# A gated long convolution inside a decoder kernel: nine block products a head, the pair products on GpSimd, the skip path from the pairs' diagonal

## The chip, the cores and the metric

The kernel runs on one core of a Trainium2 chip, as one program in one launch. The time is the device time of that program in microseconds (us). The kernel before was run three times; a profiled execution of it was taken beside them. TensorE is called PE in the profile, its weight load PEld, VectorE DVE, ScalarE ACT, GpSimd POOL and SyncE SP.

## The reference

The program is a two-layer decoder on x [8, 256, 512] (8 sequences, 256 tokens, 512 values), each sublayer followed by a residual add and a layernorm: differential attention, **a gated long convolution with the context**, a routed feed-forward of 8 experts (top 2), self attention, cross attention, routed attention. All values are float32. The change is in the second sublayer, which treats the 256 tokens as channels, 32 heads of 8, and convolves along the 512 values:

```python
def _L0_xattn_ref(v, k, bias, x1, x2, num_heads):   # v = x, x1 = x2 = context, k [32, 512]
    vr, x1r, x2r = (t.reshape(B, H, num_heads, L) for t in (v, x1, x2))
    kv = vr[:, :, :, None, :] * x2r[:, :, None, :, :]          # 8 x 8 pairs a head
    y = irfft(rfft(kv, n=2 * L) * rfft(k, n=2 * L)[None, :, None, None, :])[..., :L]
    y = y + kv * bias.reshape(H, num_heads)[None, :, :, None, None]
    return jnp.einsum('bhijl,bhil->bhjl', y, x1r).reshape(B, D, L)

x = _layernorm(x + _L0_xattn_ref(x, L0_xattn_k, fside_S2_0, ctx_2048, ctx_2048, 8))
```

The convolution is causal, so y at l is the sum over m <= l of k[l - m] times the pair at m. The `bias` term comes, after the sum over i, to c_j times the sum over i of bias_i x_i c_i.

## The kernel before

**Layout.** `long_conv` works on turned data: `xh[i]` and `ch[i]` hold x and the context for token half i as 128 partitions x 4 blocks (KB) x 8 sequences x 128 tokens, so 128 neighbouring values of L lie on the partitions and L is 4 blocks of 128. `xh[0]`, `ch[0]`, `xh[1]`, `ch[1]` reuse large buffers whose names in the profile are those of other stages (`first_h`, `w_l1a`). `turn` (helper L166) transposes the sixteen token tiles of x into `xh`: eight even ones in front of the heads, four odd ones after head 0 and four after head 1. The context is loaded from `ctx_d` in DRAM, four DMAs a half (L551).

**One head** (loop over h = 0 to 31, 16 a half). The pairs kv[k] (L571) are 128x512 products (8 sequences x 8 x 8 pairs), one for each block k of L; k = 0, 1, 2 are made on VectorE, k = 3 on GpSimd. Within 128x128 blocks the causal convolution is a lower block triangle with one Toeplitz block T0 to T3 for each distance: y_lb is the sum over k <= lb of T(lb-k) kv[k], ten block products. The blocks of a head are slices of `wt` [128, 512], which a DMA reads from the DRAM tile `filters` (L565) by an access pattern that steps back one value a row. `project` (L172) accumulates each y_lb in a PSUM bank `ps_y` (six banks); a float32 product of 128x128 by 128x512 is issued as two matmul instructions. VectorE multiplies each ps_y by the context into z (L606, three buffers) and sums over i into `yc` (L609).

**The skip path of a head.** GpSimd makes u = x c (L579) and u times bias (L580), VectorE sums over i into `us` (L587), GpSimd makes r = c us (L589), r + x (L595) and, last, x = r + yc in place (L610). These are 128x256 operations.

**The routing.** When the sixteen heads of half 0 are done, the router of the next sublayer is run for its eight token tiles between the heads of half 1: each tile is transposed back on TensorE (`pt_c`, L789), copied by ScalarE to a row tile `xn` (L795), its moments taken by VectorE (L145, L146) and normed (L771), and router logits come from `ps_r` (L178) and `pt_r` (L190). Then `choose` (VectorE: softmax, top two), `send` (L842, L843, then L856: sixteen indirect DMAs, issued on GpSimd, that write the rows to their experts' slots), `table` (L893: block tables) and `meanwhile` (the first expert blocks) follow. Half 1 is routed after head 31, beside the first expert products (`pg`, `pu` on L172).

**What sets the order.** Each engine works through its own instruction stream in order. The framework's scheduler places the instructions of all engines by a plan of its own; nothing in this stage is ordered by hand. SP issues the loads and stores of the whole program from one in-order queue. Pools with a number of buffers (`bufs`) make the next writer of a tile wait until the readers of the buffer are done.

```python
for k in range(KB):
    (nc.gpsimd if k == KB - 1 else nc.vector).tensor_tensor(kv[:, k], x_i, c_j, ALU.mult)
...
for lb in range(KB):
    project(ps, lambda k: wt[:, (lb - k) * P : (lb - k + 1) * P], lambda k: kv[:, k], n=lb + 1)
    nc.vector.tensor_tensor(z, ps, c_i, ALU.mult)
    nc.vector.tensor_reduce(yc[:, lb], z, AX.X, ALU.add)
```

Of the kernel before, what the change touches and what calls it, by code (L numbers as in the profile page):

```python
# [50 lines left out]
def decoder_kernel(ctx: ExitStack, tc: tile.TileContext, a: dict, out: bass.AP):  # L51
# [37 lines left out]
    filters = dram.tile([NH, P, KPAD], F32, tag="filters", name="filters")  # L89

# [6 lines left out]
    def spread_filters():  # L97
        n = NH // 4
        for h in range(0, NH, n):
# [3 lines left out]
            )  # L103

# [132 lines left out]
    class Pipeline:  # L237
# [3 lines left out]
        def __init__(self):  # L241
            self.steps = []
# [15 lines left out]
    def diff_attention():  # L258
# [26 lines left out]
        load_x(range(TPG, NT))  # L285
        spread_filters()
# [34 lines left out]
        clear_slots(wpool)  # L321

# [212 lines left out]
    def long_conv(router, load_experts, xh, ch, ps_t, meanwhile):  # L535
# [5 lines left out]
        with ExitStack() as st:  # L541
# [18 lines left out]
            for h in range(NH):  # L560
                i, at = divmod(h * NHEAD, P)
                hs = slice(at, at + NHEAD)
                xv, cv = xh[i], ch[i]
                wt = work.tile([P, D], F32, tag="wt", name="wt", bufs=3)
                nc.sync.dma_start(out=wt, in_=toeplitz(h))  # L565
                if h == 2:
                    load_experts()

                kv = work.tile([P, KB, B, NHEAD, NHEAD], F32, tag="kv", name="kv")
                for k in range(KB):  # L570
                    (nc.gpsimd if k == KB - 1 else nc.vector).tensor_tensor(  # L571
                        kv[:, k],
                        xv[:, k, :, hs].unsqueeze(2).broadcast_to(shape),
                        cv[:, k, :, hs].unsqueeze(3).broadcast_to(shape),
                        ALU.mult,
                    )

                u = work.tile([P, KB, B, NHEAD], F32, tag="u", name="u")
                nc.gpsimd.tensor_tensor(u, xv[:, :, :, hs], cv[:, :, :, hs], ALU.mult)  # L579
                nc.gpsimd.tensor_tensor(  # L580
                    u,
                    u,
                    sk[:, h * NHEAD : (h + 1) * NHEAD].unsqueeze(1).unsqueeze(1).broadcast_to([P, KB, B, NHEAD]),
                    ALU.mult,
                )
                us = work.tile([P, KB, B], F32, tag="us", name="us")
                nc.vector.tensor_reduce(us, u, AX.X, ALU.add)  # L587
                r = work.tile([P, KB, B, NHEAD], F32, tag="r", name="r")
                nc.gpsimd.tensor_tensor(  # L589
                    r,  # L590
                    cv[:, :, :, hs],
# [24 lines left out]
                if h == NH // 2 - 1:  # L616
                    tiles, choose, send, table = route(ps_t, xv, i)
                    for f in tiles:
                        f(work)
# [1354 lines left out]
```

## Time and profile before

| what | us |
|---|---|
| median of three runs | 2171.05 (2167.81 to 2173.65) |
| profiled execution, its own time | 2169.91 |
| its span in the profile | 2168.2 |
| convolution, first to last product | 483.18 to 782.64 |
| busy in the span: PE, DVE, ACT, POOL | 2012.0, 1275.9, 603.4, 827.9 |

The profile is of one execution. A busy share is an average over stages with different limits, so a stage is read in windows of its own. In a group line, the number after the bar is the busy time, then the mean of one in ns, then the idle time of the engine just in front of it and what ended that. The row of a matmul is longer than the distance between two starts, since they overlap. In a line of the timeline, the first number is the start in us from the start of the span, the second its length, and the brackets give the idle time before it and what released it. PEclk is the share of its full clock that TensorE was granted.

### The profile page before, as it was taken

How to read it: one execution, taken by the hardware profiler on the slowest of the kernel's cores; microseconds unless marked ns; L12 is line 12 of the kernel's file. 1: busy time of each engine (PE TensorE's matmuls, PEld its weight loads, DVE VectorE, ACT ScalarE, POOL GpSimd, SP SyncE). 2: the span in 40 equal slices, each digit the busy share in tenths (PEclk: the TensorE clock that was granted, in tenths of full speed). 3: DMA queues.
4: the chain of work that ended last, by engine and by line, in shares of the span. 5: the costliest groups of instructions: out<-in, count | busy, mean ns of one | idle time of the engine just before them, and what ended most of it. 6: DMA issues, size and time to landing. Idle time of an engine off the chain costs nothing. (4 is left out here: it accounts for less than half of the span.)

```text
span 2168.2 us, 36044 instructions
## 1 busy us (share of the span) xinstructions
PE 2012.0 (93%) x15094; PEld 1221.4 (56%) x15094; DVE 1275.9 (59%) x1935; ACT 603.4 (28%) x765; POOL 827.9 (38%) x919
## 2 busy tenths in 40 slices
PE   8979999879998999999959999999999999999995
PEld 6645655444443455566536665656877875444443
DVE  4677777658888963222244756456344343576787
ACT  4545556510010022111113333430110111333332
POOL 2677777736557622000034544333000000142343
PEclk9999999999999999999989999999999999999998
DMA  6899702235133153142141211002100100000000
GB/s 228 333 402 400 290 2 60 84 100 189 29 117 121 34 165 137 64 146 65 42 151 30 69 34 46 2 2 98 39 20 20 32 8 1 1 6 16 11 21 30
DMA packets 110033, 197.58 MB, mean 91 GB/s; under 512 B 7088, under 2 KB 30768, under 8 KB 109872
## 3 DMA queue, kind: packets, MB, share of 16 engines
q1 hardware_dynamic: 104752, 178.49, 23.3%
q0 software_dynamic: 5120, 16.78, 2.3%
q8 instruction: 121, 1.98, 0.4%
q14 instruction: 40, 0.33, 0.0%
HBM read 93.54 MB, written 112.20 MB: 95 GB/s over the span
## 5 line engine op out<-in xcount | busy, mean ns | idle before, releaser
L1357 DVE RECIPROCAL rsum<-ps_pv 128x256 f32<-128x256 f32 x128 | 224.4, 1753 | 241.2 <-PE ps_pv L1349 241.2
L172 PE MATMUL ps_y<-kv,wt 128*128 128x512 f32 x640 | 281.5, 599 | 5.7 <-POOL kv L571 2.7
L1313 ACT ACTIVATE pT<-ps_k 128x1536 f32<-128x1536 f32 x128 | 185.8, 1451 | 278.5 <-PE ps_k L1305 272.1
L1253 DVE TENSOR_REDUCE neg<-rows 128x12 f32<-128x1536 f32 x128 | 223.0, 1742 | 46.6 <-POOL rows L1244 46.6
L1314 POOL TENSOR_SCALAR_AFFINE_SELECT pT<-pT 128x1024 f32<-128x1024 f32 x128 | 141.2, 1103 | 245.8 <-ACT pT L1313 245.7
L1242 ACT COPY rows<-ps_q 128x1536 f32<-128x1536 f32 x128 | 184.2, 1439 | 175.9 <-PE ps_q L1233 123.4
L1244 POOL TENSOR_SCALAR_AFFINE_SELECT rows<-rows 128x1024 f32<-128x1024 f32 x128 | 141.8, 1108 | 231.8 <-ACT rows L1242 231.6
L172 PEld LDWEIGHTS ps_y<-kv,wt 128*128 128x128 f32 x640 | 121.3, 192 | 157.9 <-issue 139.3
L1324 POOL TENSOR_TENSOR pT<-pT 128x512 f32<-128x512 f32 x112 | 145.6, 1300 | 9.4
L205 PE MATMUL ps_f<-xT,w_l1a 128*128 128x256 f32 x512 | 127.4, 396 | 12.2 <-ACT xT L218 12.2
L1159 POOL DMA_INDIRECT w_l1x<-ys,slots x32 | 33.0, 1032 | 263.4 <-DMA ys<-y_m 255.7
L205 PE MATMUL ps_t<-w_l1f,xT 128*128 128x512 f32 x256 | 123.0, 615 | 0.0
L205 PEld LDWEIGHTS ps_f<-xT,w_l1a 128*128 128x128 f32 x512 | 95.6, 194 | 33.4 <-ACT xT L218 14.3
L1071 PE MATMUL po_m<-dn,hT 128*128 (+1 forms) x216 | 98.7, 593 | 1.0 <-ACT hT L1061 1.0
L140 POOL TENSOR_SCALAR rstd<-bn_mv 128x1 f32<-128x1 f32 x80 | 16.7, 209 | 210.0 <-DVE bn_mv L146 204.2
L1349 PE MATMUL ps_pv<-pT,ones_v 128*32 128x256 f32 (+1 forms) x1152 | 84.5, 375 | 8.2 <-POOL pT L1324 7.9
L609 DVE TENSOR_REDUCE yc<-z 128x64 f32<-128x512 f32 x128 | 86.1, 674 | 5.7 <-POOL w_l1a L610 5.3
L1233 PE MATMUL ps_q<-kz,qT 32*128 32x128 f32 x1536 | 62.2, 292 | 16.8 <-ACT pT L1313 13.4
L172 PE MATMUL pg<-gu,xT_b 128*128 x216 | 71.0, 465 | 3.8 <-ACT xT_b L218 3.8
L1233 PEld LDWEIGHTS ps_q<-kT,qT 32*128 32x128 f32 x1536 | 49.8, 190 | 42.9 <-issue 20.5
L1233 PEld LDWEIGHTS ps_q<-kz,qT 32*128 32x128 f32 x1536 | 49.8, 190 | 42.0 <-ACT pT L1313 28.0
L1050 DVE TENSOR_TENSOR h_b<-h_b,pg 128x352 f32<-128x352 f32 x36 | 18.8, 521 | 92.1 <-ACT h_b L1049 90.6
(338 smaller groups left out, 3692.0 us busy)
## 6 DMA issues: line engine op xcount, KB each, us to landing
xs<-zero SPq DMA_DIRECT2D x8, 4352.0 KB
ys<-zero SPq DMA_DIRECT2D x8, 4352.0 KB
filters<-in_L_xattn_k SPq DMA_DIRECT2D x4, 2560.0 KB
first_h<-xs SPq DMA_DIRECT2D x36, 256.0 KB
ys<-y_m SPq DMA_DIRECT2D x36, 256.0 KB
gu<-in_L_ffn_gate_up_proj SPq DMA_DIRECT2D x3, 2816.0 KB
wt<-filters SPq DMA_DIRECT2D x32, 256.0 KB
x<-in_x SPq DMA_DIRECT2D x16, 256.0 KB
```

Source lines behind the costliest of these rows:

```text
L172: nc.tensor.matmul(ps, lhsT=lhsT(k), rhs=rhs(k), start=(k == 0), stop=(k == n - 1))
L205: nc.tensor.matmul(ps[0], lhsT=lhsT(k), rhs=rhs(k), start=(k == 0), stop=(k == KB - 1))
L609: nc.vector.tensor_reduce(yc[:, lb], z, AX.X, ALU.add)
L1071: nc.tensor.matmul(po, lhsT=hT[:m, i, :], rhs=dn[i][:m, bass.ds(e, 1), :], start=(i == 0), stop=(i == len(FCH) - 1),)
L1233: nc.tensor.matmul(block[:, s, j, :], lhsT=q(rows, c, b * S + i * P, P), rhs=k(rows, c, b * S + keys * P, P), start=True, stop=True,)
L1242: nc.scalar.copy(d.rearrange("p j s k -> p s j k"), block)
L1244: nc.gpsimd.affine_select(out=rows, in_=rows, compare_op=ALU.is_ge, fill=-FAR, base=0, pattern=[[0, 8], [-1, P]], channel_multiplier=1,)
L1253: return lambda: nc.vector.tensor_reduce(neg[u // upb % 2][:, :, :, c], d, AX.X, ALU.max, negate=True)
L1313: nc.scalar.activation(p[:, 0:3].rearrange("p j s q -> p s j q"), block, AF.Exp)
L1314: nc.gpsimd.affine_select(out=p[:, 0:2].rearrange("p j s q -> p (j s) q"), in_=p[:, 0:2].rearrange("p j s q -> p (j s) q"), compare_op=ALU ...
L1324: nc.gpsimd.tensor_tensor(p[:, 3], p[:, 1], p[:, 2], ALU.add)
L1357: nc.vector.reciprocal(r, ps[:, 1, :])
```

## The change

Nine products a head take the place of ten. T2 is applied once to kv[0] + kv[1] (`both`): its result serves y2 (which needs T2 kv[0]) and y3 (which needs T2 kv[1]). It is made first, in y2's PSUM bank, ScalarE copies it to an SBUF tile `common`, and what is too much or missing is made good by products with differences of filter blocks: y2 = common + (T1 - T2) kv[1] + T0 kv[2], added in the same bank, and y3 = common + (T3 - T2) kv[0] + T1 kv[2] + T0 kv[3], where VectorE adds `common` to the finished bank in the next head's step (`last_sum`). The differences are made once from the 32 filter rows on GpSimd (`filter_changes`), spread to a DRAM tile `changes` of 8.4 MB (`spread_changes`, on SP after the zeros of `clear_slots`), and a second DMA a head loads `wd` [128, 384] (two buffers).

All four pair products of a head and the sum `both` are made on GpSimd, one head ahead (`kv` has two buffers, `both` and `common` one); head 0's pairs are on VectorE. The skip path takes the products x_i c_i from the diagonal of kv: VectorE multiplies it by the bias into `u`, 128x256 a head. Four heads form a group: one `skip_sums` on VectorE (128x1024 to 128x128) and `weighted`, `residual`, `done` on GpSimd (128x1024 each), the last three one in each of the first three steps of the next group. z has one buffer.

For heads 2 to 14 and 16 to 30 the order on PE, DVE and Pool is the written one (`manual_schedule`): `step`. The eight token tiles of half 0's routing stand one in each of steps 16 to 23, in front of the head's products; `choose`, `send`, `table` and `meanwhile` are handed to the scheduler in front of steps 24 to 27. Heads 0, 1, 15 and 31 are left to the scheduler. The loops for the odd turns stand where they stood in the source. The core of the diff:

```diff
+    changes = dram.tile([NH, P, D], F32, tag="changes", name="changes")
...
+    def filter_changes(pool):
+        f = pool.tile([NH, KPAD], F32, tag="f_rows", name="f_rows")
+        nc.sync.dma_start(out=f, in_=a["L0_xattn_k"])
+        d = pool.tile([NH, 2, S], F32, tag="f_diff", name="f_diff")
+        second = f[:, 2 * P : 2 * P + S]
+        nc.gpsimd.tensor_tensor(d[:, 0], f[:, P : P + S], second, ALU.subtract)
+        nc.gpsimd.tensor_tensor(d[:, 1], f[:, 3 * P : 3 * P + S], second, ALU.subtract)
+        return d
+    def spread_changes(d):
+        nc.sync.dma_start(
+            out=changes[:, :, :],
+            in_=d.rearrange("h j c -> h (j c)").unsqueeze(1).broadcast_to([NH, P, D]),
+        )
+    def toeplitz_changes(h):
+        flat = changes[h].rearrange("m c -> (m c)")
+        return flat[P : P + P * (D - 1)].rearrange("(m c) -> m c", c=D - 1)[:, : D - P]
...
         load_x(range(TPG, NT))
+        d_filters = filter_changes(wpool)
         spread_filters()
...
         clear_slots(wpool)
+        spread_changes(d_filters)
...
+            GH = 4
+            GT = GH * NHEAD
+            over = [P, KB, B, GT]
+            class Group:
+                def __init__(self, g):
+                    self.i, at = divmod(g * GT, P)
+                    self.hs = slice(at, at + GT)
+                    self.xg, self.cg = xh[self.i][:, :, :, self.hs], ch[self.i][:, :, :, self.hs]
+                    self.yc = work.tile(over, F32, tag="yc", name="yc")
+                def skip_products(self, head):
+                    if head.h % GH == 0:
+                        self.u = work.tile(over, F32, tag="u", name="u")
+                    same = head.kv.rearrange("p k b j i -> p k b (j i)")[:, :, :, :: NHEAD + 1]
+                    part = sk[:, head.h * NHEAD : (head.h + 1) * NHEAD]
+                    at = head.h % GH * NHEAD
+                    nc.vector.tensor_tensor(
+                        self.u[:, :, :, at : at + NHEAD],
+                        same,
+                        part.unsqueeze(1).unsqueeze(1).broadcast_to([P, KB, B, NHEAD]),
+                        ALU.mult,
+                    )
+                def skip_sums(self):
+                    self.us = work.tile([P, KB, B, GH], F32, tag="us", name="us", bufs=1)
+                    nc.vector.tensor_reduce(
+                        self.us,
+                        self.u.rearrange("p k b (n i) -> p (k b) n i", i=NHEAD),
+                        AX.X,
+                        ALU.add,
+                    )
+                def weighted(self):
+                    self.r = self.u
+                    four = [P, KB * B, GH, NHEAD]
+                    nc.gpsimd.tensor_tensor(
+                        self.r.rearrange("p k b (n i) -> p (k b) n i", i=NHEAD),
+                        self.cg.rearrange("p k b (n i) -> p (k b) n i", i=NHEAD),
+                        self.us.rearrange("p k b n -> p (k b) n").unsqueeze(3).broadcast_to(four),
+                        ALU.mult,
+                    )
+                def residual(self):
+                    nc.gpsimd.tensor_tensor(self.r, self.r, self.xg, ALU.add)
+                def done(self):
+                    nc.gpsimd.tensor_tensor(self.xg, self.r, self.yc, ALU.add)
+            class Head:
+                def __init__(self, h, group):
+                    self.h = h
+                    self.i, at = divmod(h * NHEAD, P)
+                    self.hs = slice(at, at + NHEAD)
+                    self.xv, self.cv = xh[self.i], ch[self.i]
+                    at = h % GH * NHEAD
+                    self.yc = group.yc[:, :, :, at : at + NHEAD]
+                    self.wt = work.tile([P, D], F32, tag="wt", name="wt", bufs=3)
+                    nc.sync.dma_start(out=self.wt, in_=toeplitz(h))
+                    self.wd = work.tile([P, D - P], F32, tag="wd", name="wd")
+                    nc.sync.dma_start(out=self.wd, in_=toeplitz_changes(h))
+                    self.kv = work.tile([P, KB, B, NHEAD, NHEAD], F32, tag="kv", name="kv")
+                def pairs(self, k):
+                    (nc.gpsimd if self.h else nc.vector).tensor_tensor(
+                        self.kv[:, k],
+                        self.xv[:, k, :, self.hs].unsqueeze(2).broadcast_to(shape),
+                        self.cv[:, k, :, self.hs].unsqueeze(3).broadcast_to(shape),
+                        ALU.mult,
+                    )
+                def add_pairs(self):
+                    self.both = work.tile(shape, F32, tag="both", name="both", bufs=1)
+                    nc.gpsimd.tensor_tensor(self.both, self.kv[:, 0], self.kv[:, 1], ALU.add)
+                def block(self, n):
+                    return self.wt[:, n * P : (n + 1) * P]
+                def change(self, n):
+                    return self.wd[:, n * S : n * S + P]
+                def sum_of(self, ps, *parts, first=True):
+                    if first:
+                        ps = psum.tile([P, B, NHEAD, NHEAD], F32, tag="y", name="ps_y")
+                    for k, (wb, xb) in enumerate(parts):
+                        nc.tensor.matmul(
+                            ps,
+                            lhsT=wb,
+                            rhs=xb,
+                            start=first and k == 0,
+                            stop=k == len(parts) - 1,
+                            skip_group_check=True,
+                        )
+                    return ps
+                def weighted_sum(self, lb, y):
+                    z = work.tile([P, B, NHEAD, NHEAD], F32, tag="z", name="z", bufs=1)
+                    nc.vector.tensor_tensor(
+                        z, y, self.cv[:, lb, :, self.hs].unsqueeze(2).broadcast_to(shape), ALU.mult
+                    )
+                    nc.vector.tensor_reduce(self.yc[:, lb], z, AX.X, ALU.add)
+                def products(self):
+                    kv, of, at = self.kv, self.block, self.change
+                    y2 = self.sum_of(None, (of(2), self.both))
+                    self.common = work.tile(shape, F32, tag="common", name="common", bufs=1)
+                    nc.scalar.copy(self.common, y2)
+                    y0 = self.sum_of(None, (of(0), kv[:, 0]))
+                    y1 = self.sum_of(None, (of(1), kv[:, 0]), (of(0), kv[:, 1]))
+                    self.sum_of(y2, (at(0), kv[:, 1]), (of(0), kv[:, 2]), first=False)
+                    y3 = self.sum_of(
+                        None, (at(1), kv[:, 0]), (of(1), kv[:, 2]), (of(0), kv[:, 3])
+                    )
+                    self.y = [y0, y1, y2, y3]
+                def last_sum(self):
+                    nc.vector.tensor_tensor(self.y[3], self.y[3], self.common, ALU.add)
+                    self.weighted_sum(3, self.y[3])
+            def step(h, routed=lambda: None):
+                head = heads[h]
+                before = heads[h - 1] if h % (NH // 2) else None
+                behind = heads[h + 1] if h + 1 < NH else None
+                group, at = groups[h // GH], h % GH
+                passed = groups[h // GH - 1] if h % (NH // 2) >= GH else None
+                if before:
+                    before.last_sum()
+                routed()
+                head.products()
+                if behind:
+                    behind.pairs(0)
+                    behind.pairs(1)
+                    behind.add_pairs()
+                head.weighted_sum(0, head.y[0])
+                group.skip_products(head)
+                if passed and at < 3:
+                    (passed.weighted, passed.residual, passed.done)[at]()
+                if behind:
+                    behind.pairs(2)
+                    behind.pairs(3)
+                head.weighted_sum(1, head.y[1])
+                head.weighted_sum(2, head.y[2])
+                if at == GH - 1:
+                    group.skip_sums()
+            order = {mybir.EngineType.PE, mybir.EngineType.DVE, mybir.EngineType.Pool}
+            groups = [Group(0)]
+            heads = [Head(0, groups[0])]
+            for k in range(KB):
+                heads[0].pairs(k)
+            heads[0].add_pairs()
+            parts, free = [], []
             for h in range(NH):
-                i, at = divmod(h * NHEAD, P)
-                hs = slice(at, at + NHEAD)
-                xv, cv = xh[i], ch[i]
-                wt = work.tile([P, D], F32, tag="wt", name="wt", bufs=3)
-                nc.sync.dma_start(out=wt, in_=toeplitz(h))
+                if h + 1 < NH:
+                    if (h + 1) % GH == 0:
+                        groups.append(Group((h + 1) // GH))
+                    heads.append(Head(h + 1, groups[-1]))
                 if h == 2:
                     load_experts()
-
-                kv = work.tile([P, KB, B, NHEAD, NHEAD], F32, tag="kv", name="kv")
-                for k in range(KB):
-                    (nc.gpsimd if k == KB - 1 else nc.vector).tensor_tensor(
-                        kv[:, k],
-                        xv[:, k, :, hs].unsqueeze(2).broadcast_to(shape),
-                        cv[:, k, :, hs].unsqueeze(3).broadcast_to(shape),
-                        ALU.mult,
-                    )
-
-                u = work.tile([P, KB, B, NHEAD], F32, tag="u", name="u")
-                nc.gpsimd.tensor_tensor(u, xv[:, :, :, hs], cv[:, :, :, hs], ALU.mult)
-                nc.gpsimd.tensor_tensor(
-                    u,
-                    u,
-                    sk[:, h * NHEAD : (h + 1) * NHEAD].unsqueeze(1).unsqueeze(1).broadcast_to([P, KB, B, NHEAD]),
-                    ALU.mult,
-                )
-                us = work.tile([P, KB, B], F32, tag="us", name="us")
-                nc.vector.tensor_reduce(us, u, AX.X, ALU.add)
-                r = work.tile([P, KB, B, NHEAD], F32, tag="r", name="r")
-                nc.gpsimd.tensor_tensor(
-                    r,
-                    cv[:, :, :, hs],
-                    us.unsqueeze(3).broadcast_to([P, KB, B, NHEAD]),
-                    ALU.mult,
-                )
-                nc.gpsimd.tensor_tensor(r, r, xv[:, :, :, hs], ALU.add)
-                yc = work.tile([P, KB, B, NHEAD], F32, tag="yc", name="yc")
-                for lb in range(KB):
-                    ps = psum.tile([P, B, NHEAD, NHEAD], F32, tag="y", name="ps_y")
-                    project(
-                        ps,
-                        lambda k: wt[:, (lb - k) * P : (lb - k + 1) * P],
-                        lambda k: kv[:, k],
-                        n=lb + 1,
-                    )
-                    z = work.tile([P, B, NHEAD, NHEAD], F32, tag="z", name="z", bufs=3)
-                    nc.vector.tensor_tensor(
-                        z, ps, cv[:, lb, :, hs].unsqueeze(2).broadcast_to(shape), ALU.mult
-                    )
-                    nc.vector.tensor_reduce(yc[:, lb], z, AX.X, ALU.add)
-                nc.gpsimd.tensor_tensor(xv[:, :, :, hs], r, yc, ALU.add)
+                last = h == NH // 2 - 1 or h == NH - 1
+                if h < 2 or last:
+                    step(h)
+                else:
+                    if not parts and free:
+                        free.pop(0)()
+                    with tc.manual_schedule(engines=order):
+                        step(h, parts.pop(0) if parts else lambda: None)
+                if last:
+                    heads[h].last_sum()
+                    groups[h // GH].weighted()
+                    groups[h // GH].residual()
+                    groups[h // GH].done()
                 if h < 2:
                     for t in range(h * PH + 1, (h + 1) * PH, 2):
                         turn(t)
                     if h == 1:
                         x_first.close()
                 if h == NH // 2 - 1:
-                    tiles, choose, send, table = route(ps_t, xv, i)
-                    for f in tiles:
-                        f(work)
-                    for f in (choose, send, table, meanwhile):
-                        f()
+                    tiles, choose, send, table = route(ps_t, xh[0], 0)
+                    parts = [lambda f=f: f(work) for f in tiles]
+                    free = [choose, send, table, meanwhile]
             return route(ps_t, xh[1], 1)
```

## The prediction

> **What bounds the stage now.** I read the busy shares first, then the groups by line, then the table of windows through the convolution, then the timeline around its worst gap. The changed stage is the convolution, from its first product at 483.18 us to its last at 782.64.
>
> ```profile
> PE 2012.0 (93%) x15094; PEld 1221.4 (56%) x15094; DVE 1275.9 (59%) x1935; ACT 603.4 (28%) x765; POOL 827.9 (38%) x919
> ...
> L172 PE MATMUL ps_y<-kv,wt 128*128 128x512 f32 x640 | 281.5, 599 | 5.7 <-POOL kv L571 2.7
> ```
> TensorE carries the span, and the product group waits only 5.7 us in all. The shares average over stages, so I go to the stage itself (columns: window, its length, busy time and count of PE, PEld, DVE, ACT, POOL, granted clock, DMA share, GB/s).
>
> ```profile
> 523.00:563.00 40.00, 40.00 (x100) 18.18 (x99) 35.79 (x58) 0.00 (x0) 22.45 (x27) 1.00 0.24 87
> ...
> 643.00:683.00 40.00, 36.04 (x86) 15.20 (x85) 39.82 (x117) 0.26 (x1) 22.68 (x24) 1.00 0.39 137
> 683.00:723.00 40.00, 37.26 (x81) 16.07 (x80) 30.68 (x51) 0.00 (x0) 37.00 (x44) 0.91 0.28 93
> ```
> In the plain heads TensorE never stops, VectorE has 4 us of 40 free and GpSimd 17. Only where the first half's routing is mixed in does TensorE lose time.
>
> ```profile
> 681.99 1.90 POOL L856 DMA_INDIRECT xs<-xn,slots  x1 [0.30 <-DVE kv L571]
> ...
> 689.27 0.96 POOL L856 DMA_INDIRECT xs<-xn,slots  x1 [0.30 <-issue]
> ...
> 691.51 1.07 POOL L571 TENSOR_TENSOR kv<-w_l1a 128x512 f32<-128x512 f32 x1
> 692.63 11.89 PE L172 MATMUL ps_y<-kv,wt 128*128 128x512 f32 x20 [2.74 <-POOL kv L571]
> ```
> Sixteen dispatch transfers hold GpSimd from 668.68 to 690.25, the pair product queued behind them comes late, and TensorE idles. The windows after it show the clock:
>
> ```profile
> 690.00:692.00 2.00, 0.00 (x0) 0.00 (x0) 0.98 (x2) 0.00 (x0) 1.98 (x4) 0.99 0.45 168
> 692.00:694.00 2.00, 1.36 (x2) 0.83 (x3) 2.00 (x3) 0.00 (x0) 2.00 (x3) 0.50 0.22 74
> 694.00:696.00 2.00, 2.00 (x3) 0.67 (x2) 2.00 (x4) 0.00 (x0) 2.00 (x4) 0.50 0.76 264
> 696.00:698.00 2.00, 2.00 (x4) 0.76 (x3) 0.52 (x2) 0.00 (x0) 2.00 (x4) 0.50 0.90 281
> 698.00:700.00 2.00, 2.00 (x5) 0.84 (x4) 0.00 (x0) 0.00 (x0) 2.00 (x4) 0.80 0.13 45
> ```
> After about 3.1 us of rest TensorE runs some 6 us at half clock, 3.0 us lost. A long stall costs itself plus 3 us.
>
> **1. The products.** Forty matmul instructions start in 17.43 us, 0.43 us each (a row's 592 ns overlaps the next). A block product is two, a head ten products, 8.6 us. Nine are 7.74. All four pair products, the copy and the extra add must hide behind 7.74 (below). 32 x 0.86 = **-27.5**.
>
> **2. Do the others keep up with 7.74 us a step?** GpSimd: four pairs at 1.07 (L571's row on the first half; back to back 1.02) are 4.27; `both` has no row, bounds 1.07 and L1324's 1.30 (contiguous 128x512), taken 1.30, the same shape; per four heads `weighted` 1.9, `residual` and `done` 2.35 each (the 128x256 rows, 0.63 and 0.72, scaled by L1324 to 128x1024; bounds 1.1, the affine select of that shape, and 2.55), 1.65 a head. Sum 7.2. VectorE: four multiplies (0.68) and four reduces (0.67), chained because z has one buffer: 774.09 to 774.82 is 0.73 for a chained step, so 5.8; the add into PSUM 0.73 (bounds 0.60 independent, 1.10 with twice the PSUM traffic); the skip product 0.7 (bounds 0.33, half a pair product, and 1.3, when GpSimd holds it up as it holds L571: 0.85 mean against 0.67 at best); group reduce 1.2 / 4 = 0.3. Sum 7.5. ScalarE's copy, 0.6, has 1.9 us before product five wants the bank. All hidden, so 0, but thinly: each 0.1 us over 7.74 costs 3 us, up to 32 heads. The two DMAs for `wd` and `wt` need 0.6 us each of an idle queue: 0.
>
> [...]
>
> **3. The start.** SP works in order. Before, w_l1a's four loads from ctx_d were issued at 436 us; in the built program they stand behind first_h's, released at 473.14 in both, and ahead of the first `wt`. 2.1 MB at 0.30 MB/us (the rate of first_h and `wt`: 2.36 MB in 10 us is 0.24; gu's 0.415 is the other bound): 5.1 to 8.9, taken **+6.9**. Head 0's pairs hide in it. The eight odd turns and ps_cs, 0.88 + 2.5 + 0.81 us on TensorE's timeline between heads 0 and 2 before, now lie in that wait: **-4.2**. The rest of 2.6 to 4 us may halve the clock: 0 to 3, taken **+1.5**. The write of `changes` (8.4 MB at 11.3 us per 4.35 MB, 22 us) ends well before cx is used (75 us of cover): 0; f_rows and two subtractions stand before GpSimd's first busy stretch: 0.
>
> **4. The half boundary.** In the built order VectorE meets head 15's skip product and the group reduce in the middle of step 14, in front of z2. That product waits for GpSimd's fourth pair of head 15, which cannot start before head 13 frees its kv buffer: pairs, `both`, `done` and pairs end 8.1 us into the step, VectorE was free at 5.1. z2 then ends at 11.5, 3.8 into step 15; y1 of head 15 takes z2's bank and is due at 1.7: 2.05 stall, and product five waits 0.4 for the copy behind the late add: 2.45. Then tile 0's transpose stands on TensorE between heads 15 and 16 and waits for `done` of the group, which waits for last_sum(15). VectorE ends z2's reduce 4.5 into step 15, last_sum(14) (add, multiply, reduce) at 6.7, three multiplies and reduces at 11.1, last_sum(15) at 13.3; `done` takes 2.35, so 15.7. TensorE is through at 7.74 + 2.45 = 10.2: 5.5 idle, less 0.57 that the same transpose waited before, plus 3.0 of clock. **+10.4**. Head 31 repeats the 2.45 on its way in; its long tail lies beside an expert's 6.1 us of products: **+2.4**.
>
> **5. Dispatch and routing.** Now the sixteen transfers stand between the third and fourth pair of head 27. They begin 7.0 us into step 26, take 20.3 (1.27 each), and the pair 1.07: 28.4 into step 26. TensorE has products up to 7.74 + 6.9 = 14.6: idle 14. Then `both` of head 28 needs two more pairs and itself: +2. Clock +3, the chained tail on VectorE 1.3, and steps 16 to 23, where the norm (0.69 + 0.18 + 0.55 a tile) comes on top of VectorE's 7.5, 1.5 (they get 1.3 us of transposes as well). 21.8, against 1.16 + 0.53 + 0.58 + 0.76 + 0.86 + 2.74 + 3.0 = 9.6 before, all of which goes. **+12.2** (0 if the transfers start 14 us earlier; 16 if slots come 3 us late).
>
> [...]
>
> **Sum.** -27.5 + 6.9 - 4.2 + 1.5 + 10.4 + 2.4 + 12.2 = +1.7. On the profiled execution's 2169.91 (span 2168.2) that is 2171.6; it lies 1.1 below the median 2171.05 of the runs, so 2172.8 in the runs. No change is 2164.5 to 2177.6, 0.3% of the median, about what a measurement of this kernel can tell.
>
> **Rivals.**
> *The stalls stay as short as before.* If `slots` are ready a step earlier than GpSimd gets to them, or the transfers start behind less of the pairs, part 5 costs its old 9.6, and the rest under 3 us at the start keeps the clock: 2172.8 - 12.2 - 1.5 = 2159. For it: the queue of the plain heads has 17 us of 40 free on GpSimd. Against: the order is written out, and the fourth pair of head 27 stands behind all sixteen. With the boundary's clock loss gone too, 2156.
> *GpSimd becomes the bound.* Pairs at L1324's 1.30 instead of 1.07 make its step 7.2 + 0.9 = 8.1; with contention like L571's second-half mean of 1.17 on top of wide rows at 2.55, 8.0 to 8.4. It decides from 7.74; 8.3 costs 0.56 x 30 = 17, 2172.8 + 17 = 2190; 8.0 gives 2181. For it: 1.17 is already a mean of the trace, and GpSimd would be busy 93%. Against: VectorE's three pair products, the partners that slow L571 today, are gone from the plain heads.
> *VectorE's 7.5 passes 7.74* by a skip product at 1.3: +0.36 x 30 = 11, 2184, the same side, counted with the second.
>
> **How the numbers follow.** Forecast 0.42 (2164 to 2180 by the bounds of parts 3 to 5: of it 0.02 under 2164.5, 0.34 no change, 0.06 above), short stalls 0.28 (2152 to 2166: 0.25 faster, 0.03 same), an elementwise engine as the bound 0.30 (2176 to 2195: 0.27 slower, 0.03 same). Faster 0.27, same 0.40, slower 0.33. The range takes the forecast and most of both: 2155 to 2189.
>
> **What would show it.** First product near 490 us; 7.74 us between heads 3 and 14 with TensorE full in a 40 us window; VectorE above 37 and GpSimd above 36 of 40 there; a wait of some 2 us on VectorE at head 15; a transpose waiting about 5.5 us for `done` at head 16, clock 0.50 after it; some 14 us of idle at head 27's last product, ended by GpSimd's pair. Wrong: a plain step above 7.9 us (the second rival), or a dispatch gap under 5 us (the first).

## The result, and the profile after

The changed kernel takes 2184.75 us (median of 6 runs, 2179.88 to 2189.83) against 2170.07 for the kernel before (6 runs): ratio 1.0063, 95% interval 1.0045 to 1.0080. It is slower by 14.7 us; the forecast was 2172.8, inside a range of 2155 to 2189. The profiled execution took 2185.6, its span is 2183.8, 15.6 more than before. All stretches below are cut from the two spans. One run of e2 below took 3706.95 us at a granted clock of 0.758, a state that no other run here shows, and is left out of its median and ratio.

The page has the same lines as before, now with two groups for the products:

```profile
PE 2001.3 (92%) x15030; PEld 1217.3 (56%) x15030; DVE 1282.8 (59%) x1883; ACT 622.1 (28%) x797; POOL 893.4 (41%) x909
...
L671 PE MATMUL ps_y<-kv,wt 128*128 128x512 f32 x384 | 188.7, 614 | 9.5 <-POOL kv L650 9.5
...
L671 PE MATMUL ps_y<-kv,wd 128*128 128x512 f32 x128 | 68.7, 619 | 12.4 <-ACT common L692 12.4
```
640 product instructions have become 576 (the 64 on `both` are a third group). The two groups are put down with 22 us of waiting where there were 5.7, for GpSimd's pairs and for a copy on ScalarE that the kernel before does not have. The mean of one rose from 599 to 614 ns and more, a sign that some ran at a lower clock: two in a row take 1.02 us at 642.78, where PEclk is 1.00, and 2.08 at 753.43, where it is 0.50.

The windows through the stage, in the columns of before:

```profile
523.00:563.00 40.00, 39.36 (x92) 17.20 (x91) 38.10 (x52) 2.92 (x5) 35.87 (x30) 1.00 0.21 58
...
643.00:683.00 40.00, 40.00 (x117) 18.53 (x116) 38.52 (x63) 5.99 (x11) 33.30 (x34) 1.00 0.29 87
683.00:723.00 40.00, 33.22 (x86) 14.31 (x85) 39.23 (x69) 3.64 (x7) 33.12 (x30) 0.91 0.30 95
723.00:763.00 40.00, 26.66 (x52) 11.06 (x51) 28.91 (x73) 1.76 (x3) 32.96 (x33) 0.79 0.50 166
```
In the plain heads the plan nearly holds: TensorE is the fullest by its busy share, and GpSimd at 35.9 of 40 lies under it. VectorE's 38.1, however, is already full: from 511 to 613 us no gap before one of its instructions is over 0.11 us, and over heads 5 to 12 it takes 7.96 us a head, where TensorE's own work takes 7.73. The token tiles between 643 and 683 cost TensorE no wait at all. In the next 80 us it loses 20 us, and its clock with it. The timeline there shows two different stalls. The first:

```profile
713.14 2.34 POOL L630 TENSOR_TENSOR u<-u,w_l1a 128x1024 f32<-128x1024 f32 x1
713.30 2.27 DVE L778 TENSOR_TENSOR fm<-fm,idx_e 128x64 f32<-128x64 f32 x1
715.85 0.73 DVE L781 TENSOR_TENSOR o<-idx_e,fm_at 128x64 f32<-128x64 f32 x1
716.51 0.69 DVE L702 TENSOR_TENSOR ps_y<-ps_y,common 128x512 f32<-128x512 f32 x1
717.31 0.58 ACT L692 COPY common<-ps_y 128x512 f32<-128x512 f32 x1 [7.93 <-DVE ps_y L702]
717.94 2.07 PE L671 MATMUL ps_y<-kv,wd 128*128 128x512 f32 x2 [5.70 <-ACT common L692]
```
VectorE works through the small operations of `choose` (L778, L781) between its sums; the add of the last head's `common` (L702) comes late, the one buffer of `common` is not free until then, ScalarE, idle for 7.93 us, can only then begin this head's copy, and TensorE's fifth product waits 5.70 for the copy. The second is the one that was forecast:

```profile
751.32 0.96 POOL L1001 DMA_INDIRECT xs<-xn,slots  x1 [0.30 <-issue]
752.30 3.11 POOL L650 TENSOR_TENSOR kv<-w_l1a 128x512 f32<-128x512 f32 x3
753.43 2.08 PE L671 MATMUL ps_y<-kv,wt 128*128 128x512 f32 x2 [9.52 <-POOL kv L650]
756.94 2.08 PE L671 MATMUL ps_y<-both,wt 128*128 128x512 f32 x2 [1.43 <-POOL both L659]
```
The sixteen transfers (732.05 to 752.28) stand in front of head 27's fourth pair: 9.52 us, then 1.43 for `both` of head 28. The windows behind it show what the rest does to the clock:

```profile
744.00:748.00 4.00, 0.00 (x0) 0.00 (x0) 0.00 (x0) 0.00 (x0) 3.09 (x4) 1.00 0.86 262
748.00:752.00 4.00, 0.00 (x0) 0.00 (x0) 0.00 (x0) 0.00 (x0) 3.08 (x4) 0.57 0.59 223
752.00:756.00 4.00, 2.08 (x2) 0.50 (x2) 2.59 (x2) 0.00 (x0) 3.98 (x7) 0.50 0.23 88
756.00:760.00 4.00, 3.06 (x4) 1.51 (x5) 3.93 (x6) 0.59 (x1) 4.00 (x5) 0.50 0.67 204
760.00:764.00 4.00, 4.00 (x8) 1.49 (x8) 3.83 (x6) 0.00 (x0) 3.92 (x3) 0.72 0.36 124
```
The grant falls to a half while TensorE still rests and stays there until 762, 13.7 us in all.

The half boundary shows its two forecast waits, at heads 15 and 16:

```profile
618.01 1.28 PE L671 MATMUL ps_y<-kv,wd 128*128 128x512 f32 x2 [2.27 <-ACT common L692]
...
629.00 1.07 PE L934 MATMUL pt_c<-ident,first_h 128*128 128x128 f32 x4 [4.72 <-POOL first_h L633]
```

**Where the 15.6 us are.** Four marks that both kernels have cut the spans: the turn behind the rest for `first_h` (473.78 before, 475.55 after), the first transpose of the routing (628.20, 629.00), the first turn of an expert's rows, right behind the last product (782.48, 794.77), the end.

| stretch | before | after | difference | the sum had |
|---|---|---|---|---|
| up to the stage | 473.8 | 475.6 | +1.8 | 0 |
| start and heads 0 to 15 | 154.4 | 153.5 | -1.0 | -2.2 |
| routing and heads 16 to 31 | 154.3 | 165.8 | +11.5 | +3.8 |
| the rest | 1385.7 | 1389.0 | +3.3 | 0 |

In the two middle rows TensorE rests 10.9 us before and 35.3 after. Its busy time inside the stretches in which the granted clock was 0.50, halved, is what the low clock cost: 4.7 us before, 18.2 after. So 24.3 us of added rest drew 13.6 us of added clock loss behind it; against that stand the 27.5 us of products that are gone. Together that is +10.4, and the two rows add up to +10.5.

### The profile page after: what moved, and what is told of

Read it like the earlier page. It is cut to its first block, busy times and chain, and to the rows that moved or that the text cites. A ratio compares the mean times of both kernels' runs of the same rounds, so it can differ in the third digit from the quotient of the medians.

```text
span 2183.8 us, 36165 instructions
## 1 busy us (share of the span) xinstructions
PE 2001.3 (92%) x15030; PEld 1217.3 (56%) x15030; DVE 1282.8 (59%) x1883; ACT 622.1 (28%) x797; POOL 893.4 (41%) x909
## 3 DMA queue, kind: packets, MB, share of 16 engines
q8 instruction: 121, 1.98, 0.4%
## 5 line engine op out<-in xcount | busy, mean ns | idle before, releaser
L671 PE MATMUL ps_y<-kv,wt 128*128 128x512 f32 x384 | 188.7, 614 | 9.5 <-POOL kv L650 9.5
L671 PEld LDWEIGHTS ps_y<-kv,wt 128*128 128x128 f32 x384 | 76.0, 199 | 106.7 <-issue 87.2
L1494 PE MATMUL ps_pv<-pT,ones_v 128*32 128x256 f32 (+1 forms) x1152 | 84.8, 375 | 8.3 <-POOL pT L1469 7.9
L671 PE MATMUL ps_y<-kv,wd 128*128 128x512 f32 x128 | 68.7, 619 | 12.4 <-ACT common L692 12.4
L692 ACT COPY common<-ps_y 128x512 f32<-128x512 f32 x32 | 18.7, 585 | 207.8 <-DVE ps_y L702 108.9
L650 POOL TENSOR_TENSOR kv<-first_h 128x512 f32<-128x512 f32 x60 | 66.9, 1137 | 25.3 <-PE ps_y L671 15.9
```

What stands on the lines that cost most here:

```text
L671: nc.tensor.matmul(ps, lhsT=wb, rhs=xb, start=first and k == 0, stop=k == len(parts) - 1, skip_group_check=True,)
```

## The experiments

The ratios are to runs of the kernel before on the same chip. e1, e3, e4 and e9 are one run each.

**e1, the filter changes alone.** On the kernel before:

```diff
+        d_filters = filter_changes(wpool)
         spread_filters()
...
         clear_slots(wpool)
+        spread_changes(d_filters)
```


> The kernel before, with only the filter rows' load, the two subtractions and the 8.4 MB write of `changes` added, which nothing reads. Theory (the write crowds the queues from which TensorE's instructions come): between 245 and 295 us TensorE shows rests put down to `issue`, 1.5 to 2 us in all, and the attention stage ends that much later, give or take one clock window. Rival (the 1.8 us by which the changed kernel reaches the stage late is clock chance alone): no such rests, less than 0.3 us in that stretch, and the total within 0.2% of before.

The waits for `issue` came where the theory put them. The changed kernel's timeline, then e1's:

```profile
244.82 11.19 SPq L119 DMA_DIRECT2D changes<-f_diff  x1
256.06 37.55 SPq L414 DMA_DIRECT2D cx<-in_ctx  x2
...
272.48 0.94 PE L196 MATMUL ps_v<-w_l,xT 128*128 128x128 f32 x6 [0.91 <-issue]
...
282.71 0.64 PE L1494 MATMUL ps_pv<-pT,ones_v 128*32 128x256 f32 x7 [0.27 <-issue]
```

```profile
269.47 0.94 PE L191 MATMUL ps_v<-w_l,xT 128*128 128x128 f32 x6 [0.84 <-issue]
...
279.70 0.64 PE L1370 MATMUL ps_pv<-pT,ones_v 128*32 128x256 f32 x7 [0.27 <-issue]
```
The kernel before has none there. Counting GpSimd's mask operations, the 80th begins 4.23 us earlier in e1 than before and the 88th only 2.37 earlier: 1.86 us go in this stretch, and 1.93 in the changed kernel, 1.1 to 1.2 of them in the two waits. The write keeps the DMA engines at least 0.9 busy from 256 to 298 us, 42 us for the 22 of the forecast, at a little over 200 GB/s for most of it. The page of the changed kernel lists two DMA queues of the kind `instruction` (1.98 and 0.35 MB); that the write holds up their transfers fits the word `issue` but is argued, not shown. The rest of the row up to the stage (e1 gained 4.2 us before 150 us, the changed kernel 1.3) lies elsewhere: in the changed kernel at places where the half clock was 3.4 us shorter or longer than before (3.4 us from 124 for 6.8 from 122, 6.8 from 383 for 3.4 from 385). For e1 no view shows the clock there. The total is 2171.19, beside a median of 2167.19 for the kernel before.

**e2, ten products again, all else as changed.**

```diff
-                    y2 = self.sum_of(None, (of(2), self.both))
...
+                    y2 = self.sum_of(None, (of(2), kv[:, 0]), (of(1), kv[:, 1]), (of(0), kv[:, 2]))
...
-                    nc.vector.tensor_tensor(self.y[3], self.y[3], self.common, ALU.add)
```


> The changed kernel with ten products a head again: no `both`, no `common`, no added bank; all else (GpSimd pairs, groups, written order, wd's loads unused) as changed. Theory (TensorE is still the bound of the plain steps, VectorE and GpSimd that of the routing steps): heads 1 to 15 go from 7.73 to 8.6 us a step, 13 us longer, the steps with routing grow by less than 0.4 us each, total 14 to 20 us above the changed kernel, about 2201. Rival (the elementwise engines are the bound throughout): less than 5 us above, under 2190.

Median 2199.36 of three runs, ratio 1.0143 (1.0114 to 1.0171): 14.6 us above the changed kernel's median, 17 by the two ratios. The products saved are worth 15 to 17 of the 27.5 us. The plain step is 8.58 us with TensorE busy without a pause, so the rival, an elementwise engine as the bound throughout, is out.

The trace of e2 shows something more. Its steps are as long as those of the kernel before, it has neither `both` nor `common`, and yet both stalls of the routing are there, the first at `send`'s own product:

```profile
728.67 0.66 PE L985 MATMUL ps_pl<-o,before 128*128 128x64 f32 x2 [6.76 <-DVE o L977]
...
759.95 45.62 PE L671 MATMUL ps_y<-kv,wt 128*128 128x512 f32 x100 [11.34 <-POOL kv L650]
```
From head 16's first product to the last product's end it takes 169.5 us, 32 more than sixteen of its plain steps.

**e3 and e4, the routing of half 0 behind head 31.** e3 on the changed kernel, e4 on the one before:

```diff
-                    parts = [lambda f=f: f(work) for f in tiles]
-                    free = [choose, send, table, meanwhile]
+            for f in tiles:
+                f(work)
+            for f in (choose, send, table, meanwhile):
+                f()
             return route(ps_t, xh[1], 1)
```


> The changed kernel with the whole routing of half 0 moved behind head 31, where it is exposed; the total is therefore longer and not compared, the convolution is. Theory (what the second half loses comes from the routing between the heads): heads 16 to 31 at 7.73 us a step apart from some 1 us in the first step of a group, 124 to 130 us from head 16's first product to the last product (166 in the changed kernel from the transpose on), clock 1.00. Rival (VectorE or GpSimd is over 7.74 in steps without routing as well): 134 us or more.

> The kernel before with the same move. Theory: heads 16 to 31 at 8.6 us, 137 to 139 us, so that without routing the change gains 8 to 13 us in this half, where it lost 11.5 with it. Rival: the half takes 145 us or more because VectorE, 35.8 of 40 us busy, is over its share there too.

From head 16's first product to the last product's end e3 takes 129.9 us, and e4 137.5. e3's step is 7.73, about 8.64 at heads 8, 12, 24 and 28, with the clock at 1.00 from head 16 until head 31. Over all 32 heads:

| first product to the first transpose behind the last | routing between the heads | behind them | the routing adds |
|---|---|---|---|
| before, e4 | 299.3 | 279.0 | 20.3 |
| changed, e3 | 302.0 | 261.8 | 40.2 |

With the routing out of the way nine products gain 17 us in the stage, and in total e3 (2190.13) beats e4 (2201.0) by 11. The same routing costs twice as much between the changed heads. That settles the place: neither the products nor the plain steps, but what the routing finds there. The shorter step is not the main thing that it finds. From head 16 on the routing adds 20 us before (157.8 for e4's 137.5), 35 in the changed kernel (165.1 for e3's 129.9), and 32 in e2, whose step is the old one. Most of the added cost came with the rest of the change, which e2 keeps: all pairs on GpSimd one head ahead, in the written order. Which part of that it is, e2 does not separate; e10 below points to the pairs.

**e5, the pairs behind the dispatch on VectorE** (head 27's fourth, all of head 28 and its `both`).

```diff
-                    (nc.gpsimd if self.h else nc.vector).tensor_tensor(
+                    (nc.vector if self.h in (0, 28) or (self.h, k) == (27, 3) else nc.gpsimd).tensor_tensor(
```


> The changed kernel with the products that are queued behind the sixteen dispatch transfers, the fourth pair of head 27 and all of head 28 with its `both`, on VectorE. Theory (GpSimd's queue behind the transfers makes the stall at head 27's last product): the 9.5 us rest and the 1.4 behind it fall below 2 us together, and the four half-clock windows after them (13.7 us, about 5 us lost) to at most one; VectorE gets 4.5 us more work in a stretch in which it is full, so the total falls by 8 to 14 us. Rival (VectorE's routing work is the bound there anyway): it falls by less than 4.

Ratio 1.0039 (1.0027 to 1.0051), about 5 us better by the ratios, whose intervals just overlap, and between the two expectations:

```profile
756.82 2.07 PE L673 MATMUL ps_y<-both,wt 128*128 128x512 f32 x2 [3.97 <-POOL both L659]
```
One rest of 3.97, for head 29's `both`, stands in place of 9.52 and 1.43, but VectorE gives part of it back as waits of 1.59 and 2.85 at head 31, and the half clock only moves (6.8 us behind 755, 6.8 behind 782).

**e6, heads 15 and 31 in the written order.**

```diff
-                if h < 2 or last:
+                if h < 2:
                     step(h)
```


> The changed kernel with heads 15 and 31 in the written order too, so that their skip product no longer stands in front of the head before's z2. Theory: VectorE's 1.3 us wait in steps 14 and 30 and TensorE's 2.3 us wait for `common` at heads 15 and 31 go; but the group's reduce, `weighted` and `residual` now come after head 15's sums, so `done` is later by up to 6 us and the transpose behind it waits longer: total between 5 lower and 5 higher. Rival (the early product costs nothing, the 2.3 us come from VectorE's rate): the waits for `common` stay at 2.3.

```profile
628.09 1.11 PE L934 MATMUL pt_c<-ident,first_h 128*128 128x128 f32 x4 [9.67 <-POOL first_h L633]
```
The waits of 2.3 us at heads 15 and 31 are gone, so the early skip product made them. The transpose now waits 9.67 for `done` instead of 4.72, as the group's tail comes later. Ratio 1.0051 (1.0033 to 1.0069): no difference from the changed kernel that these intervals can tell.

**e7, the start as it was**: context loads of w_l1a first, odd turns in the written order behind heads 0 and 1.

```diff
-            for i in range(2):
+            for i in (1, 0):
...
+                    with tc.manual_schedule(engines=order):
+                        step(h)
+                        for t in range(h * PH + 1, (h + 1) * PH, 2):
+                            turn(t)
```


> The changed kernel with w_l1a's context loads issued in front of first_h's, and the odd turns in the written order behind heads 0 and 1 on TensorE, as they stood before. Theory: first product at 480 to 484 us instead of 492.8, turns cost 4 us again between heads 0 and 2, the 10.2 us at half clock there shrink by a window or two: 5 to 9 us lower in total. Rival (the load order is hidden by the turns' copies, which are needed anyway): less than 2 us.

```profile
486.63 2.08 PE L671 MATMUL ps_y<-both,wt 128*128 128x512 f32 x2 [5.63 <-POOL both L659]
...
532.85 2.04 PE L671 MATMUL ps_y<-kv,wd 128*128 128x512 f32 x2 [5.46 <-DMA wd<-changes]
```
The first product starts 6.2 us earlier, but waits 5.63 for `both`, which nine products need at once. The turns cost 3 us again, and head 4 waits 5.46 for its `wd`, whose load is late. Ratio 1.0095 (1.0077 to 1.0113), 7 us worse. The theory named the wrong bound of the start, and in the end cost more than it brought.

**e8, half 0's norms on ScalarE.**

```diff
-                    nc.vector.tensor_scalar(
-                        r, r, mv[:, i, 0:1], rstd[:, i : i + 1], ALU.subtract, ALU.mult
+                    nc.scalar.activation(
+                        r, r, AF.Identity, bias=nb, scale=rstd[:, i : i + 1]
```


> The changed kernel with the norm of half 0's eight token tiles (VectorE, 0.84 us each) on ScalarE, which is busy 15 of 166 us there; VectorE keeps a 128x1 product a tile. Theory (from the first transpose of the routing on VectorE is the bound: 143.3 us busy where TensorE has 132 us to do at full clock): steps 17 to 24 fall from 8.2 to 9.3 us to about 8, total 3 to 7 us lower. Rival (the losses are single stalls, not VectorE's sum): steps unchanged and less than 2 us.

Ratio 1.0063 (1.0041 to 1.0084), nothing. Steps 17 to 22 keep their 8.16 to 9.25 us: they are TensorE's own 7.73 with 0.43 for a tile's transposes and 1.09 more where the logits' products are. Only steps 23 and 24 shrink, and the stalls behind them take the gain. VectorE's sum over the half is not the bound while the tiles run; the theory fell.

**e9, `choose`, `send`, `table` and `meanwhile` behind head 31**, the tiles left in place.

```diff
-                    free = [choose, send, table, meanwhile]
+                    later = [choose, send, table, meanwhile]
```


> The changed kernel with the eight token tiles of half 0 still in steps 16 to 23, but `choose`, `send`, `table` and `meanwhile` behind head 31, where their work and the transfers are exposed; the total is longer and not compared, the convolution is. Theory (the tiles cost little, choosing on VectorE and dispatching on GpSimd cost the rest): from head 16's first product steps 16 to 23 stay at 8.2 to 9.4, steps 24 to 31 fall from 8.6 to 20 us to 7.73 (one of 8.6, and 2.3 us at head 31), the half to 137 to 141 us from the first transpose, 25 to 29 less than in the changed kernel. Rival (the tiles' norms leave VectorE behind and the backlog is what is paid from step 25 on): steps 24 to 27 stay above 8.6 without choosing too.

From the first transpose to the last product's end 140.2 us, 25.7 less than in the changed kernel. The tiles' steps from head 17 on are unchanged, head 24 still takes 9.0, heads 25 to 30 take 7.7 to 7.8, but for head 28's 8.9. So the eight tiles cost the convolution little, and choosing and dispatching cost it 26 us: the two stalls with the low clock that follows them.

**e10 to e12, a hybrid.** Nine products in heads 0 to 23; ten in heads 24 to 31, which then need neither `both` nor `common`, with pairs 0 and 1 on VectorE (all four for heads 27 and 28). e11 also begins the tiles one step later; e12 keeps only pair 0 on VectorE.

```diff
+                        if self.h in (0, 27, 28) or self.h >= 24 and k < 2
...
+                    if self.h >= 24:
+                        self.y = [
+                            self.sum_of(None, *[(of(lb - k), kv[:, k]) for k in range(lb + 1)])
+                            for lb in range(KB)
+                        ]
+                        return
...
+                    parts = [lambda: None, *(lambda f=f: f(work) for f in tiles[:6])]
+                    parts.append(lambda: [f(work) for f in tiles[6:]])
```


> Nine products in heads 0 to 23 as changed, ten in heads 24 to 31, with pairs 0 and 1 of those heads on VectorE and 2 and 3 on GpSimd (all four on VectorE for heads 27 and 28), so that no product there waits for ScalarE's copy of `common`, TensorE has 8.6 us a head to cover choosing and dispatching, and GpSimd has 4 us a head free for the transfers. Theory (the route stretch loses through chains over VectorE, ScalarE and GpSimd for which 7.73 us is too short a cover): the 5.7 us wait goes, the dispatch wait falls below 4, the stretch of heads 24 to 31 takes 75 to 82 us (97 in the changed kernel), total 12 to 20 us below the changed kernel, 2165 to 2173. Rival (VectorE's choosing blocks heads whatever their products): a wait of 4 us or more remains at heads 25 and 26 and the total is within 8 us of the changed kernel.

> The hybrid with the token tiles of half 0 one step later (none in step 16, two in step 23). Theory (the rest between heads 15 and 16 is the first transpose waiting for `done`, and nothing else is behind it): the 5.2 us wait and its clock window go, heads 15 and 16 take 19 to 21 us instead of 26.9, total 4 to 7 us below the hybrid, at or below the kernel before. Rival (GpSimd is still busy with the group's tail and head 16's pairs, so TensorE waits for `both` instead): a wait of 3 us or more at head 16's first product, less than 2 us in total.

> The same with only pair 0 of heads 24 to 26 and 29 to 31 on VectorE (pair 1 on GpSimd too). Theory (VectorE, 76.6 of 79 us busy there, is now the bound of heads 24 to 31): the last eight heads take 3 to 6 us less, total 2 to 5 us below e11. Rival (GpSimd's queue around the transfers is as close): the dispatch wait comes back, 4 us or more in front of a product of heads 27 to 30, and no gain.

| | median us | ratio to before | interval | heads 15 and 16 | heads 24 to 31 |
|---|---|---|---|---|---|
| changed | 2184.75 | 1.0063 | 1.0045 to 1.0080 | 27.2 | 95.3 |
| e10 | 2166.83 | 1.0017 | 1.0002 to 1.0032 | 26.9 | 78.7 |
| e11 | 2166.13 | 1.0014 | 1.0000 to 1.0027 | 21.6 | 84.8 |
| e12 | 2159.29 | 0.9974 | 0.9964 to 0.9984 | 21.5 | 79.4 |

e10 takes back most of the loss, 10 us by the ratios. No product waits for the dispatch any more, and the one long rest left in the last eight heads, 6.25 us, is `send`'s own matmul waiting for `choose`. It takes both halves of the hybrid: those heads take 93.3 us in e2, with ten products alone, 91.3 in e5, with only the pairs behind the dispatch on VectorE, and 78.7 in e10. e11 shortens the 5.2 us rest at the half boundary to 1.0 as expected and loses as much in the last eight heads, where VectorE then holds up `z` (1.76 and 2.18 us of rest on TensorE) and its pairs (0.19, 0.77 and 0.66). e12 gives VectorE one pair less, and the gain arrives:

```profile
694.00:734.00 40.00, 32.03 (x79) 14.55 (x78) 38.53 (x107) 0.26 (x1) 21.82 (x18) 0.91 0.32 101
734.00:774.00 40.00, 40.00 (x97) 17.79 (x95) 38.01 (x56) 0.00 (x0) 29.29 (x25) 1.00 0.29 102
```
TensorE is full through the dispatch at full clock; only the rest for `choose` remains. e12 beats both kernels: 0.26% faster than the one before.

## Why the prediction held in its range and was 12 us short

The measured time lies in the range and in the case that got 0.33. It did not come by the mechanism that was put in that case: in the plain steps GpSimd (35.9 of 40) did not pass TensorE, and VectorE, which did (7.96 us a head for 7.73), cost 3.7 us in all. It came by the forecast's own stalls, one of which was missed. The likeliest case, no change at 0.40, did not come, and that the time still fell into the range is in part luck.

- **Products, -27.5.** Right: 7.73 us a plain head for 8.6, and 15 to 17 us of total by e2.
- **The cover, 0.** Nearly. The rows fit (`both` 1.29 for 1.30, `weighted` 1.96 for 1.9, `residual` 2.35, the add 0.69 for 0.73), but the skip product took 1.16 us, 1.36 in heads 5 to 12, not 0.7. So VectorE's step was 7.96, not 7.5, as in the last of the rivals. VectorE falls behind, and after a group's reduce the copy of `common` comes 0.65 us late; such a head takes 8.64. Four heads, 3.7 us in all (e3).
- **The write of `changes`, 0.** Wrong: 42 us for 22, and TensorE lost 1.9 us beside it, most of it in waits for `issue` (e1). The cover of cx's first use was not the only thing that it stood beside.
- **The start, +4.2.** First product at 492.80 for the forecast 490, by another cause: no product waited for `wt`. The odd turns, which the forecast counted as a gain, were the bound, each waiting for a copy on VectorE or ScalarE, at half clock:

```profile
484.00:488.00 4.00, 1.54 (x6) 1.14 (x7) 4.00 (x5) 0.58 (x1) 4.00 (x4) 0.72 1.21 291
488.00:492.00 4.00, 3.23 (x17) 2.83 (x15) 1.88 (x4) 0.58 (x1) 1.01 (x1) 0.50 1.17 313
492.00:496.00 4.00, 4.00 (x9) 2.29 (x9) 0.33 (x2) 0.58 (x1) 1.07 (x1) 0.50 1.05 400
```
  The half clock lasted 10.2 us, 4.4 us lost where 1.5 was taken.
- **The half boundary, +10.4.** Right, by its steps: 2.27 at head 15 for 2.45, 4.72 at the transpose for 5.5, 3.4 us lost to the clock, in two stretches, for 3.0. e6 takes away the first wait (and lengthens the second), e11 most of the second.
- **Dispatch and routing, +12.2.** This step failed. The transfers behaved as forecast (7.9 us into step 26 for 7.0, 20.2 us long), and their rest was shorter, 9.5 and 1.4 for 14 and 2, because step 26 itself had become 12.7 us long. What was left out is `choose`. The sum gave VectorE 1.5 us for the norms and nothing for the some forty small operations that follow, though it had put VectorE at 7.5 of 7.74 a step: 5.70, 1.39 and 1.00 us of rest and two more stretches of half clock (6.8 and 3.4 us). The views of before had shown VectorE 39.82 of 40 busy in that window. 3.9 of the 9.6 us that the sum counted there were waits for VectorE (1.16, 0.53, 0.58, 0.76 and 0.86); it treated all as gone, where these grew.
- **Clock.** Two stalls at 3.0 us each, less one of before, and 1.5 at the start, 4.5 in all, were forecast; 13.6 us came. Rests of 1 to 10 us followed one another through the routing, each long one with its stretch of half clock. The rest in the kernel before that the prediction put at about 3.1 us is 2.74 in its own row, and the 2.27 us at head 15 drew 3.4 us of half clock as well.
- **The rest, 0.** +3.3: the first expert blocks wait 4.42 us for a copy (2.96 before) and have 6.8 us of half clock for 3.4. What made this rest longer was not tried.

## What to carry to other kernels

When a change moves work between engines, list everything that is interleaved with their steps and cost it against the slack that every one of them has left, not by what it lost under the old form: here the same routing cost 20 us before and 40 in the changed kernel, and a longer TensorE step alone did not bring that back (e2). Where slack is needed only in some steps, keep the heavier form of the products there and lighten the other engines too (e10, e12). A busy share under one can already be a full engine: VectorE's 38.1 of 40 left gaps of at most 0.11 us. And a one-buffer tile written by a third engine can turn a late elementwise operation into a TensorE stall, which the clock then lengthens: here 5.70 us for `common`, with 6.8 us of half clock.

## What the runs showed of the hardware

- The half clock comes in whole pieces. In the traces of the kernel before and the changed one its stretches are 3.41, 6.83, 10.24, 13.65 and 20.48 us, that is one, two, three, four and six times 3.413, nothing between; e9 has one of 37.55, eleven times. Only the last stretch, at the end of a trace (10.53 and 10.59 us), is no multiple. What sets the number of pieces is not shown: in the changed kernel a rest of 2.27 us drew one, 4.72 one, 5.70 two, 9.52, followed by work with a 1.43 us gap in it, four, and 16.8 six, where 2.74 us in the kernel before drew two.
- A small VectorE operation that reads two SBUF tiles can take ten times its time beside GpSimd. `fm` (L778) took 2.27 us beginning 0.16 us after the start of a 2.34 us GpSimd product, and 0.21 us at 719.64 with GpSimd at rest; the reduce behind it (L780), which reads one tile, took 0.22 beside a pair product on GpSimd and 0.21 without. The skip product ranges from 0.60 (720.50, GpSimd at rest) to 2.40 (753.41, through five GpSimd instructions in a row). Beside the long GpSimd instructions, `residual` and `done` of 2.35 us, it took 1.68 to 1.95. What makes it wait is not shown.
- A DMA write of 8.4 MB, which in e1 nothing reads, cost TensorE 1.9 us in another stage (1.86 in e1, 1.93 in the changed kernel).
